# Two scheduling edits in a sparse masked attention kernel: projection units at an even step across the turns of the batch pairs, and the first query block of batches 0 and 1 computed in the last pair's slots

## The chip, the cores and the metric

The kernel runs on one NeuronCore of a Trainium2 chip, in one launch. The metric is device microseconds of one execution, the median of several runs. All data is float32, except for a bfloat16 mask bias of one block.

## The reference, cut to what matters

The input `x` is 8 batches of 2048 rows by 256 columns, `adj` a 2048 x 2048 sparse matrix whose first rows and columns are by far the fullest. Layer 0 is a graph convolution with two linear maps and two batch norms, a residual and a layer norm. Layer 1, which the change concerns, is attention masked by `adj`:

```python
qkv = h @ W                                  # 256 -> 3 x 256
q, k, v = ...                                # 4 heads of 64
mask = where(adj == 0, -inf, 0.0)
scores = einsum('bhid,bhjd->bhij', q, k) / sqrt(64) + mask
out = softmax(scores) @ v
# layer 1
x = _layernorm(x + out, axis=-1)
```

## The kernel before

Layer 0 ends at 957 us of the profiled execution with its output `y_d` in DRAM, not yet normalized. Everything below is `attention()`.

**Batches go in four pairs** (0 and 1, 2 and 3, and so on). A pair needs two kinds of work.

The first is **projection**, in 8 *units* of 512 rows, `(b, c)`: two batches of four chunks. A unit loads `y` and `x` (`load`, two SP DMAs of 512 KB each), applies the second batch norm (`bn`, ACT), turns `y` on the PE (`turn_y`), adds it to `x` and takes layer norm statistics (`norm`, DVE), makes scale and shift (`root` on POOL, `shift` on DVE), applies them (`apply`, ACT), turns the result (`turn` on PE, `turned` on ACT), and multiplies by the weights in four tiles of 128 rows (`keys_values`, `queries`). ACT copies the products out of PSUM (`took_keys_values`, `took_rows`). `store` (SP) writes 1032 KB of keys and values to `kv_d[p]` and 512 KB of queries to `q_d[p]`, one DRAM tensor of each for each pair.

Within a unit lies the pair's **first-block** work. The first 128 query rows of a batch are attended densely, as their rows of `adj` are the fullest. `first_queries` makes those queries transposed in `q0`, whose other halves POOL sets to zero by `memset`. Then for each of the unit's tiles: `turn_keys`, `turned_keys`, `scores0` (a mask bias and two products, PE), `exps0` (ACT), `weigh` (products with the values, added up in the one PSUM tile `po0` over the 16 tiles of a batch). At the end of a batch come `finish` (DVE), `residual` (POOL) and `out_stats` (DVE) for block 0.

The second is the **group loop**, for the query blocks `t` of 1 to 15. There are 132 groups in a pair, 528 in all. For each, POOL gathers 128 rows of keys and values of both batches (`gather`, `kg`, 528 KB) and, in 40 of 132 groups, 128 rows of queries (`qg`). DVE multiplies and reduces (`score`: `pr`, then `s`), ACT takes exponentials (`exps`, `pw`), `weigh_values` multiplies the values by them (`wv`; on ACT in two of five groups, in the last pair in three of five; else on DVE), and PE adds up (`add_up`, into `po`). After the last group of a block come `finish`, `residual` and `out_stats`, and after every fourth block `out_root`, `out_shift` and `emit`, which writes 512 KB of output.

The order on all five engines is the program's order, engine by engine; nothing is rearranged. Group `n` has a *slot* in which `score(n + 5)`, `exps(n + 4)`, `weigh_values(n + 3)`, `add_up(n)` and `gather(n + 10)` are issued, and behind them what is planned for the slot: the dictionary `slots` for projection of the next pair, `later` for the ends of blocks.

- Pair 0 is projected ahead of the loop, with `projection(0, 9)`: units follow at a step of 9 slots, which there are only an order, as no groups lie between.
- In pair p's 132 slots, pair p + 1 is projected with `projection(p + 1, 14)`: unit k begins at slot 14k, so that its last product is in slot 118 and its last `store` in slot 120. The first gather of pair p + 1 is in slot 122 and reads what the stores wrote.
- The last pair's slots hold no projection.

`kg` has 10 buffers, `wv` 5, `pr` 2, `x1` (the residual rows, kept from `load` to `emit`) 15, `ps_m` (PSUM for all of projection) 4, `ps_o` (for `po`) 3.

Of the kernel before, what the change touches and what calls it, by code (L numbers as in the profile page):

```python
# [8 lines left out]
F32 = mybir.dt.float32  # L9
# [4 lines left out]
AF = mybir.ActivationFunctionType  # L14
# [24 lines left out]
def tile_gcn_then_masked_attention(  # L39
# [15 lines left out]
    nc = tc.nc  # L55
    ENG = mybir.EngineType
    PSUM = bass.MemoryType.PSUM
    P = 128
    B, N, D = x.shape
    H = w1t.shape[1]  # L60
    O = w2t.shape[1]
    HD = D // NHEADS
# [790 lines left out]
    def rows(b, k, src, n=CH):  # L853
        return src[b, k * n : (k + 1) * n, :].rearrange("(t p) d -> p t d", p=P)
# [39 lines left out]
    def attention():  # L894

        with ExitStack() as st:
# [7 lines left out]
            x1, yt, x1t, ln, lo, kvr, qr, kt, q0, s0, p0, po0, zs, pms = ({} for _ in range(14))  # L904
# [58 lines left out]

            def first_queries(b):

                pm = pms["q0", b] = ps_m.tile([P, HP, P], F32, name="pm")
                for hp in range(HP):
                    for d in range(ND):
                        nc.tensor.matmul(
                            pm[:, hp, :], wq[:, d, hp * P : (hp + 1) * P], x1t[b, 0][:, d, :P],  # L970
                            start=(d == 0), stop=(d == ND - 1),
                        )
                q0[b] = ip.tile([P, HP, 2, P], F32, name="q0")
                for r in range(2):
                    nc.gpsimd.memset(q0[b][(1 - r) * HD : (2 - r) * HD, :, r, :], 0.0)

            def took_queries(b):
                pm = pms.pop(("q0", b))
                for r in range(2):
                    rs = slice(r * HD, (r + 1) * HD)  # L980
                    nc.scalar.activation(q0[b][rs, :, r, :], pm[rs], AF.Copy, scale=HD**-0.5)
# [97 lines left out]
            def residual(b, t):  # L1079
                c, i = divmod(t, TPC)  # L1080
                xt = x1[b, c]
                nc.gpsimd.tensor_add(xt[:, i, :], zs.pop((b, t)), xt[:, i, :])  # L1082

            def out_stats(b, t):
                c, i = divmod(t, TPC)
                if not i:
                    lo[b, c] = LayerNorm(ip, x1[b, c], "lo", 8)
                lo[b, c].stats([i])

            def out_root(b, c):  # L1090
                lo[b, c].root(range(TPC))

            def out_shift(b, c):
                lo[b, c].shift(range(TPC))

            def emit(b, c, half):
                lo[b, c].apply(range(IT * half, IT * (half + 1)))
                if half:
                    del lo[b, c]
                    nc.sync.dma_start(rows(b, c, out), x1.pop((b, c)))  # L1100

            def projection(p, step):

                slots = {}

                def at(s, f, *args):
                    slots.setdefault(s, []).append((f, args))

                units = [(b, c) for b in range(p * G2, (p + 1) * G2) for c in range(NCH)]
                for k, (b, c) in enumerate(units):  # L1110
                    s = k * step
                    at(max(0, s - step), load, b, c)
# [9 lines left out]
                    if not c:  # L1122
                        at(s + 9, first_queries, b)
                        at(s + 10, took_queries, b)
                    for i in range(TPC):
                        u = s + 9 + (step * i) // TPC
                        at(u, keys_values, b, c, i)
                        at(u + 1, took_keys_values, b, c, i)
                        at(u + 1, queries, b, c, i)
                        at(u + 2, took_rows, b, c, i)  # L1130
                        at(u + 2, turn_keys, b, c, i)
                        at(u + 3, turned_keys, b, c, i)
                        at(u + 4, scores0, b, c, i)
                        at(u + 5, exps0, b, c, i)
                        at(u + 7, weigh, b, c, i)
                    at(u + 3, store, b, c)
                    if c == NCH - 1:
                        at(u + 8, lambda b=b: finish(b, 0, po0.pop(b)))
                        at(u + 9, residual, b, 0)
                        at(u + 11, out_stats, b, 0)  # L1140
                return slots

            slots = projection(0, 9)
            for s in range(max(slots) + 1):
                for f, args in slots.get(s, ()):
                    f(*args)
# [32 lines left out]
            def score(n):  # L1179
# [3 lines left out]
                pr = ep.tile([P, G2, D], F32, name="pr")  # L1183
# [55 lines left out]
            def at(n, f, *args):  # L1239
                later.setdefault(n, []).append((f, args))  # L1240

            NALL_G = NP * NG
            for n in range(LEAD):
                gather(n)
# [6 lines left out]
            slots = {}  # L1251
            for n in range(NALL_G):
                p, g = divmod(n, NG)
                t, r, _, _ = tiles[g]
                if not g:
                    slots = projection(p + 1, 14) if p + 1 < NP else {}
# [11 lines left out]
                for f, args in slots.pop(g, ()):  # L1268
                    f(*args)
                for f, args in later.pop(n, ()):  # L1270
                    f(*args)
# [12 lines left out]
                assert g < NG - 1 or not slots  # L1284
            add_up(NALL_G - 1, 1)
            for n in sorted(later):
                for f, args in later[n]:
                    f(*args)
# [371 lines left out]
```

## Time and profile before

| | |
|---|---|
| Median of 3 runs | 2410.26 us (2410.09 to 2415.58) |
| The profiled execution's own time | 2455.75 us |
| Its span, from first to last instruction | 2453.9 us |
| Mean granted TensorE clock | 0.92 |
| Layer 1 begins (first `load`) | 957.8 us |
| First reduce of a score (`s`, L1186) of pair 0, 1, 2, 3 | 1152.2, 1482.8, 1819.1, 2151.0 us |
| Last reduce of a score | 2428.6 us |
| First gather (`kg`, L1168) of pair 0, 1, 2, 3 | 1144.9, 1474.8, 1811.2, 2143.5 us |

The table's lower half gives the stages: 194.4 us from the first load to the first score, then 330.6, 336.3, 331.9 and 277.6 us for the four pairs, then 25.3 us to the end. The profile is of one execution that is itself 45 us longer than the median; all sums over stages are in its time. Busy shares over the whole span mix layer 0, projection alone, loop with projection and loop without, so stages are read one by one.

### The profile page before, as it was taken

What the parts mean: (1) busy time and instruction counts of PE and PEld (TensorE: products, weight loads), DVE (VectorE), ACT (ScalarE), POOL (GpSimd) and SP (SyncE); (2) the same over time, 40 slices, a digit from 0 to 9 for tenths busy, and PEclk for the clock granted to TensorE, in tenths of its full rate; (3) what the DMA queues carried; (4) which work ended last, traced back from release to release, by engine and by line L of the source; (5) the groups of instructions that cost most, each with busy time, mean ns of one, the idle gap of its engine ahead of it and who ended that gap; (6) DMA issues with size and microseconds to landing.
All of it is one profiled execution on the core that took longest, in us unless ns stands there. A gap on an engine that the chain in (4) does not pass through costs nothing.

```text
span 2453.9 us, 28310 instructions
## 1 busy us (share of the span) xinstructions
PE 2089.6 (85%) x7860; PEld 1329.2 (54%) x7860; DVE 1911.3 (78%) x3650; ACT 1267.7 (52%) x3817; POOL 1480.1 (60%) x1497
## 2 busy tenths in 40 slices
PE   5898989888889997997899996999978999956654
PEld 1443434344434443775677774677756777744443
DVE  6977988778896665112888988888988889889996
ACT  6221111111105553554667776677757777767775
POOL 3405767576226774002767777667777668688784
PEclk7898999899899998998999998999989999978777
DMA  7868799697546743335879989899998899889995
GB/s 304 307 228 337 265 321 351 234 332 279 193 161 272 265 158 133 130 112 196 311 286 352 350 305 322 314 341 325 339 332 324 301 355 358 306 298 314 341 321 171
DMA packets 236152, 689.99 MB, mean 281 GB/s; under 512 B 25680, under 2 KB 91728, under 8 KB 213456
## 3 DMA queue, kind: packets, MB, share of 16 engines
q0 software_dynamic: 109248, 442.68, 50.5%
q1 hardware_dynamic: 124432, 228.62, 25.5%
q10 hardware_dynamic: 2304, 16.78, 1.7%
q8 instruction: 65, 1.06, 0.2%
q14 instruction: 103, 0.84, 0.1%
HBM read 557.19 MB, written 130.81 MB: 280 GB/s over the span
## 4 chain that ended last, share of the span: by engine, by line
PE 44%; DVE 14%; issue 7%; POOL 7%; ACT 5%; DMA 2%; another core or an unknown queue 1%; DVEq 0%; ACTq 0%; POOLq 0%; SPq 0%
PE pm L986 11%; PE po L1226 9%; PE pa L737 7%; DVE pr L1184 4%; PE pm L1035 3%; PE po L1054 3%; POOL kg L1168 3%; PE pa L645 3%; PE ph L498 2%; DVE s L1186 2%; ACT wv L1210 2%; DVE wv L1215 2%; ACT x L887 1%; DMA qg<-q_d,idxq 1%; POOL qg L1174 1%
## 5 line engine op out<-in xcount | busy, mean ns | idle before, releaser
L1168 POOL DMA_INDIRECT kg<-kv_d,idx x528 | 568.3, 1076 | 183.9 <-issue 107.7
L1226 PE MATMUL po<-wv,ident 128*128 128x260 f32 x1472 | 439.5, 416 | 173.5 <-DVE z L1075 87.5
L1210 ACT ACTIVATE wv<-kg,pw 128x65 f32<-128x65 f32 x1896 | 478.5, 338 | 8.8 <-remote 3.3
L1226 PEld LDWEIGHTS po<-wv,ident 128*128 128x128 f32 x1472 | 288.5, 207 | 264.1 <-issue 135.9
L1186 DVE TENSOR_REDUCE s<-pr 128x8 f32<-128x512 f32 x528 | 362.2, 686 | 34.6 <-ACT pw L1195 0.2
L986 PE MATMUL pm<-wq,x1t 128*128 128x512 f32 (+1 forms) x1024 | 377.8, 493 | 0.0
L645 PE MATMUL pa<-e,wt 128*128 128x512 f32 x536 | 264.8, 644 | 20.6 <-DVE e L353 13.0
L1184 DVE TENSOR_TENSOR pr<-qb,kg 128x512 f32<-128x512 f32 x368 | 257.3, 699 | 10.2 <-DMA kg<-kv_d,idx 9.6
L1195 ACT ACTIVATE pw<-s,padb 128x8 f32<-128x8 f32 x528 | 157.0, 300 | 201.4 <-DVE s L1186 163.3
L1215 DVE TENSOR_TENSOR wv<-kg,pw 128x520 f32<-128x520 f32 x291 | 214.0, 735 | 49.0 <-PE po L1226 20.2
L986 PEld LDWEIGHTS pm<-wq,x1t 128*128 128x128 f32 x1024 | 188.8, 192 | 82.3 <-issue 67.7
L1226 PE MATMUL po<-wv,oh 128*128 128x260 f32 x640 | 209.3, 427 | 10.3 <-DVE wv L1215 6.1
L1174 POOL DMA_INDIRECT qg<-q_d,idxq x160 | 161.0, 1006 | 48.8 <-issue 47.6
L645 PEld LDWEIGHTS pa<-e,wt 128*128 128x128 f32 x536 | 108.0, 208 | 151.4 <-issue 123.2
L1082 POOL TENSOR_TENSOR x<-z,x 128x256 f32<-128x256 f32 x128 | 122.8, 961 | 98.5 <-DVE z L1075 85.7
L563 POOL DMA_INDIRECT e<-xs_d,idx x116 | 125.2, 1079 | 81.5 <-PE pa L645 35.3
L309 POOL DMA_INDIRECT av<-in_adj_dram,fidx x116 | 134.6, 1161 | 47.8 <-issue 28.7
L1226 PEld LDWEIGHTS po<-wv,oh 128*128 128x128 f32 x640 | 133.4, 216 | 43.7 <-issue 12.4
L374 ACT COPY e<-ph 128x512 f32<-128x512 f32 x32 | 18.6, 582 | 249.1 <-PE ph L369 188.4
L931 DVE TENSOR_TENSOR x<-pm,x 128x512 f32<-128x512 f32 x64 | 43.9, 686 | 127.7 <-PE pm L925 116.3
L1054 PEld LDWEIGHTS po<-kvr,p 128*128 128x128 f32 x1024 | 137.0, 196 | 10.5 <-issue 3.8
L1035 PE MATMUL pm<-q,kt 128*128 128x256 f32 x512 | 133.7, 384 | 1.9 <-ACT kt L1023 1.9
(202 smaller groups left out, 3757.9 us busy)
## 6 DMA issues: line engine op xcount, KB each, us to landing
kv_d<-kvr SPq DMA_DIRECT2D x32, 1032.0 KB
e<-h_d SPq DMA_DIRECT2D x28, 1024.0 KB
e<-in_adj_dram SPq DMA_DIRECT2D x16, 1024.0 KB
xt<-in_x_dram SPq DMA_DIRECT2D x16, 1024.0 KB
xs_d<-xt ACTq DMA_DIRECT2D x16, 1024.0 KB
y_d<-y SPq DMA_DIRECT2D x32, 512.0 KB
yt<-y_d SPq DMA_DIRECT2D x32, 512.0 KB
x<-in_x_dram SPq DMA_DIRECT2D x32, 512.0 KB
```

Of the source, the lines that this page charges most:

```text
L645: nc.tensor.matmul(pa[c], w, xg[n].t[:, c * CH : (c + 1) * CH], start=(k == 0), stop=(k == count - 1),)
L737: nc.tensor.matmul(py, w[:, f, :], t[:, f, :], start=(f == 0), stop=(f == 1))
L986: nc.tensor.matmul(pm, x1t[b, c][:, d, i * P : (i + 1) * P], rhs(d), start=(d == 0), stop=(d == ND - 1),)
L1035: nc.tensor.matmul(pm[:, hp].rearrange("p r q -> p (r q)"), k[:, hp, :], q0[b][:, hp].rearrange("p r q -> p (r q)"), start=False, stop=Tru ...
L1054: nc.tensor.matmul(po0[b][:, h, :], p[:, h, :], heads(kvr[b, c][:, i, D:])[:, h, :], start=(j == 0 and h == 0), stop=(j == NT - 1), skip_g ...
L1168: nc.gpsimd.indirect_dma_start(out=kg[n].rearrange("p b e -> p (b e)"), out_offset=None, in_=kv_d[p][:], in_offset=bass.IndirectOffsetOnAx ...
L1174: nc.gpsimd.indirect_dma_start(out=qg[n].rearrange("p b e -> p (b e)"), out_offset=None, in_=q_d[p][:], in_offset=bass.IndirectOffsetOnAxi ...
L1184: nc.vector.tensor_mul(pr, q, kg[n][:, :, :D])
L1186: nc.vector.tensor_reduce(s.rearrange("p b h -> p (b h)"), pr.rearrange("p b (h e) -> p (b h) e", e=HD), AX.X, ALU.add,)
L1210: nc.scalar.activation(wv[n][:, b, hs], k[:, b, D:][:, hs], AF.Copy, scale=w[:, b, h : h + 1],)
L1215: nc.vector.tensor_mul(wv[n].rearrange("p b (h e) -> p b h e", e=VW), k[:, :, D:].rearrange("p b (h e) -> p b h e", e=VW), w[:, :, :, None ...
L1226: nc.tensor.matmul(po[p, t, b].rearrange("p h e -> p (h e)"), oh[n] if e >= 0 else ident, wv[n][:, b, :], start=(r == 0), stop=(r == ELL[t ...
```

## The change

1. `projection` takes a list of starting slots and plans into the one dictionary `later`, which now also has slots below 0 (in order, ahead of the loop). Pair 0's units start at slots -80, -74, ... -38, a step of 6. The units of pair p (1 to 3) start at `(p - 1) * 132 + int(88 - 16.5 * (7 - k))`: -27, -11, 5, 22, 38, 55, 71 and 88 within the pair's stretch, so 16 or 17 slots apart, and without a pause from one pair to the next. The last store is in slot 112 where it was in slot 120. `load` comes 8 slots ahead of a unit instead of one step.
2. The first 10 gathers are issued in slot -19, behind the last store of pair 0 (slot -22) and among the first unit of pair 1, whose `first_queries`, with the `memset` of `q0`, is in slot -18.
3. Pair 0 is projected without first-block work. `left_over` does that work later, from slot 382 (14 slots before the last pair's first) in steps of 15 slots: each unit's keys and values are read back from `kv_d[0]` (`read_keys_values`, 1032 KB), the 128 query rows of each batch from `q_d[0]` (`read_queries`, 128 KB) and turned on the PE (`turn_queries`), then `first_block` as before. It is done by slot 516.
4. Because the output rows of block 0 of batches 0 and 1 are then late, POOL copies their residual rows aside (`keep_rows`, into `rest`), `emit` leaves them out, and `emit_rest` writes them.
5. `pr` goes from 2 buffers to 1.

Its core (the parts that only pass names along are left out):

```diff
+            def keep_rows(b):
+                rest[b] = ip.tile([P, 1, D], F32, name=f"rest{b}", bufs=1)
+                nc.gpsimd.tensor_copy(rest[b][:, 0, :], x1[b, 0][:, 0, :])
+
+            def read_keys_values(b, c):
+                kvr[b, c] = ip.tile([P, TPC, KW], F32, name="kvr")
+                g = b % G2
+                nc.sync.dma_start(
+                    kvr[b, c],
+                    kv_d[b // G2][c * CH : (c + 1) * CH, g * KW : (g + 1) * KW].rearrange(
+                        "(t p) e -> p t e", p=P
+                    ),
+                )
+
+            def read_queries(b):
+                g = b % G2
+                zs[b, "q"] = ip.tile([P, D], F32, name="z", bufs=4)
+                nc.sync.dma_start(zs[b, "q"], q_d[b // G2][:P, g * D : (g + 1) * D])
+
+            def turn_queries(b):
+                pm = pms["q0", b] = ps_m.tile([P, HP, P], F32, name="pm")
+                rows_q = zs.pop((b, "q"))
+                for hp in range(HP):
+                    nc.tensor.transpose(pm[:, hp, :], rows_q[:, hp * P : (hp + 1) * P], ident)
+                open_queries(b)
...
+            def first_block(at, u, b, c, i):
+
+                at(u, turn_keys, b, c, i)
+                at(u + 1, turned_keys, b, c, i)
+                at(u + 2, scores0, b, c, i)
+                at(u + 3, exps0, b, c, i)
+                at(u + 5, weigh, b, c, i)
+                if c == NCH - 1 and i == TPC - 1:
+                    at(u + 6, lambda: finish(b, 0, po0.pop(b)))
+                    at(u + 7, residual, b, 0)
+                    at(u + 9, out_stats, b, 0)
+
+            def left_over(at, s0, step):
+
+                for k, (b, c) in enumerate((b, c) for b in range(G2) for c in range(NCH)):
+                    s = s0 + k * step + 6
+                    at(s - 6, read_keys_values, b, c)
+                    if not c:
+                        at(s - 6, read_queries, b)
+                        at(s - 2, turn_queries, b)
+                        at(s - 1, took_queries, b, 1.0)
+                    for i in range(TPC):
+                        first_block(at, s + (step * i) // TPC, b, c, i)
...
-            def projection(p, step):
+            def projection(at, p, starts, step, ahead):
...
-                for k, (b, c) in enumerate(units):
-                    s = k * step
-                    at(max(0, s - step), load, b, c)
+                for s, (b, c) in zip(starts, units):
+                    at(s - ahead, load, b, c)
...
-                    if not c:
+                    if p and not c:
                         at(s + 9, first_queries, b)
...
-                        at(u + 2, turn_keys, b, c, i)
-                        at(u + 3, turned_keys, b, c, i)
-                        at(u + 4, scores0, b, c, i)
-                        at(u + 5, exps0, b, c, i)
-                        at(u + 7, weigh, b, c, i)
+                        if p:
+                            first_block(at, u + 2, b, c, i)
...
-                pr = ep.tile([P, G2, D], F32, name="pr")
+                pr = ep.tile([P, G2, D], F32, name="pr", bufs=1)
...
+            NUNITS = G2 * NCH
+            FIRST, STEP0, LAST = -80, 6, 88
+            steady = NG / NUNITS
+            projection(at, 0, [FIRST + STEP0 * k for k in range(NUNITS)], STEP0, STEP0)
+            for p in range(1, NP):
+                starts = [
+                    (p - 1) * NG + int(LAST - steady * (NUNITS - 1 - k)) for k in range(NUNITS)
+                ]
+                projection(at, p, starts, int(steady), 8)
+            left_over(at, (NP - 1) * NG - 14, 15)
+            GATHER = FIRST + STEP0 * NUNITS + 13
...
+            for n in range(min(later), 0):
+                side_tasks(n)
+                if n == GATHER:
+                    for m in range(LEAD):
+                        gather(m)
```

## The prediction, on record before the change was run

> **What bounds the kernel now.** I read the layer 1 stages one by one, first by a table of stretches: the first pair's projection alone, then the four pairs between the first score of each and the next (columns: length, then busy time of PE, PE weight loads, DVE, ACT and POOL, granted clock, DMA share, GB/s).
>
> ```profile
> 1000.00:1050.00 50.00, 50.00 (x262) 37.19 (x261) 10.46 (x33) 26.78 (x65) 4.86 (x20) 1.00 0.33 110
> 1050.00:1100.00 50.00, 50.00 (x269) 37.92 (x268) 8.71 (x26) 30.39 (x73) 3.53 (x13) 1.00 0.37 126
> ...
> 1700.00:1750.00 50.00, 49.60 (x242) 38.48 (x241) 47.35 (x98) 41.53 (x142) 39.81 (x49) 1.00 1.02 387
> ```
> ```profile
> 1152.00:1483.00 331.00, 297.60 (x1388) 227.70 (x1389) 288.07 (x589) 233.26 (x800) 232.43 (x264) 0.95 0.90 326
> 1483.00:1819.00 336.00, 300.99 (x1409) 232.08 (x1409) 293.81 (x607) 238.83 (x816) 238.50 (x273) 0.95 0.91 328
> 1819.00:2151.00 332.00, 296.95 (x1409) 228.06 (x1408) 293.39 (x608) 237.79 (x816) 241.07 (x272) 0.97 0.91 326
> 2151.00:2429.00 278.00, 168.27 (x528) 123.78 (x526) 252.41 (x485) 198.61 (x783) 219.13 (x215) 0.75 0.91 312
> ```
>
> Projection alone is PE and nothing else: 50 of 50 us, DVE and DMA mostly idle. In the first three pairs, PE, DVE and DMA are all near 90%; in the last, DVE and DMA still are, while PE has over 100 us to spare. The chain that ended last, in order of time, shows the unit's beat (time, length, work):
>
> ```profile
> 985.55 2.58 PE pm L986 x8
> ...
> 1006.29 2.58 PE pm L986 x8
> ...
> 1027.03 2.58 PE pm L986 x8
> ```
>
> A unit takes 20.74 us. Later in the chain the same work returns at 1373.56 and 1443.44, four half units or 28 slots apart: 69.9 us, 2.50 us a slot. Last, the timelines of POOL and DVE where the loop begins (start, length):
>
> ```profile
> 1144.89 1.09 POOL L1168 DMA_INDIRECT kg<-kv_d,idx  x1 [0.16 <-issue]
> ...
> 1162.00 0.94 POOL L1168 DMA_INDIRECT kg<-kv_d,idx  x1 [0.30 <-issue]
> ```
> ```profile
> 1151.51 0.69 DVE L1184 TENSOR_TENSOR pr<-qb,kg 128x512 f32<-128x512 f32 x1 [6.11 <-DMA kg<-kv_d,idx]
> ```
>
> PE's projection ends near 1140; the stores land, the first ten `kg` with four `qg` take POOL 18 us, and DVE starts 12 us after PE's end.
>
> **What the skill says.** The Trainium skill, "Perfetto Trace Analysis", section Optimization Strategy: where regimes with different most-contended engines follow one another, interleaving them may help. That is the table above. The section Identifying the Most-Contended Engine says that matmul busy time misleads, since matmuls are pipelined; here the groups of the first projection sum to 208 us of matmul in a stretch of 178, so I price PE by start to start. "VectorE: DVE Perf Modes", The DRAIN you can't avoid: a wait between two DVE operations is free. The trace differs: a reduce and the multiply behind it, without a wait, are 0.60 us apart, a multiply and the reduce that waits for it 0.72. "DMA: Bandwidth & Descriptors", Issuing engines are not separate DMA queues: all share the 16 engines, so SP's re-reads compete with POOL's gathers.
>
> **Prices on PE**, start to start at full clock, from the trace's starts: 512 columns 0.43 us, 256 columns 0.216, mask bias 0.216, transposes 0.109, 65 columns 0.105. Projection proper of a unit: 16 x 0.43 + 16 x 0.216 + 16 x 0.109 = 12.1 us. First-block work: 8 x 0.109 + 4 x 0.216 + 16 x 0.216 + 32 x 0.105 = 8.55, and 0.9 for `first_queries` of a batch. Together 20.9 on average, against a beat of 20.74. A group's four `add_up` records: 4 x 0.219 = 0.88.
>
> **Step 1, the start.** Taken from the PE-bound stretch: 8 x 8.55 + 2 x 0.9 = 70.2 us. Put into it, from pair 1: the whole unit of slot -27 (20.9) and of the unit at -11 the turns and the first tile (1.7 + 2.6). Net -45 us. Short units have less filler (ACT needs 9.5 of every 12.1 us): I add 5 (0 to 12). Alone this puts PE's end at 1100, and as the first gathers now overlap with pair 1's unit, the first score at about 1103.
>
> A new wait stands against that. Slot -19 puts the gathers ahead of slot -18's `memset` of `q0` on POOL, and `scores0` in slot -14 needs it. Pair 0's last product comes at 985.5 + 8 x 12.1 - 9 (done by then) + 5 = 1078. From the last store's issue (1138.55) to the first gather (1144.89) it was 6.3 us, so the gathers start near 1087 and hold POOL for 18 us, to 1105. PE gets to `scores0` near 1087 and stands until 1106. Behind it in PE's order are `turn_y` of the next unit and so its `norm`, which DVE must do ahead of the first score. The first score comes at about 1116. Bounds: 1103 if nothing is waited for, 1127 if stores land late and the short units cost 12. I take 1116: **gain 36** (25 to 49).
>
> **Step 2, the first three pairs.** Spread evenly, PE needs 20.8 / 16.5 + 0.88 = 2.14 us a slot; at 14 slots it was 20.8 / 14 + 0.88 = 2.36 and took 2.50. So PE at the same efficiency would run at 2.26. DVE was busy for 875 us in 396 groups and keeps that, but for 1.4 units of 3.3 us that move ahead; at the 94.5% of its fullest window it needs 870 / 0.945 = 921, or 2.33 a group. DMA: 0.91 x 2.52 = 2.29. So DVE comes next, close above the others, and three in-order queues so near each other lose more than one: I take 2.39, so 946 us for the present 999: **gain 53** (30 to 75). The pause at each pair's end (132nd gather at 1466.1, next at 1474.8, where 2.4 us is usual) goes with it, as the last store is in slot 112 and the gather that needs it in 122.
>
> **Step 3, the last pair.** Added: PE 8 x 8.55 + 1, or 69 us, into more than 100 of slack. ACT: eight times 4 x (0.37 + 0.59) = 31 us, beside 199 of 278. DVE: two `finish` and `out_stats`, 2.4 us, which the start no longer has. SP: 8 re-reads of 1032 KB and 2 of 128, at 387 GB/s for a share of 1.02 some 22 us of DMA time; the share is 0.91 of 278, so it fits if the gathers leave no holes, and I charge 8 (0 to 22). POOL: four `memset` of 0.3 us. The two 0.7 us copies and the output writes of the rows kept apart are too small to show. The wait at this pair's start saves 5. **Loss 3** (gain 5 to loss 17). The work ends in slot 516 of 528, so the 25 us behind the last score stay.
>
> **Step 4, one `pr`.** A multiply may have to wait for the reduce before it, at 0.72 to 0.78 instead of 0.60. Only 71 of 528 multiplies follow the reduce directly; elsewhere another operation lies between. 71 x 0.18 = 13 at most, nothing if no wait is set. I take **5**. Step 2's cover, DVE, is full, so this is paid.
>
> **Sum:** 36 + 53 - 3 - 5 = 81 us, on a span of 2453.9. The profiled execution (2455.75) is 1.9% longer than the median of the runs shown (2410.26), so 81 becomes 79: **2331 us**. The parts' bounds do not all fall on one side: 2298 to 2366.
>
> **Rivals.**
> - *The loop does not speed up*, since PE was not what held it: DVE and DMA are as full as PE in the table. Then only steps 1 to 4 without 53 remain, and with 8 more for fuller DMA in the last pair: 36 - 3 - 5 - 8 = 20, 2390. Against it: 2.10 us a group in the last pair at the same DMA share.
> - *Everything fits*: no wait at the start (49), DVE at 94.5% throughout (78), nothing lost in the last pair: 127 less, 2285. For it: 1700 to 1750, where DVE, PE and DMA are all full at once.
> - *Slower: gather packets lengthen.* The place is the 16 DMA engines in the loop. From the queue part of the page, 50.5% of 16 x 2453.9 us over 109,248 packets is 181 ns a packet; one ns on the loop's 528 x 128 `kg` packets is 4.2 us. The loop needs 0.91 x 1276 + 22 = 1183 us of engine time. To end 7 us behind today, with 36 gained at the start, it would have to last 1276 + 36 + 7 = 1319, which takes 136 us more, or 32 ns a packet: from 213 ns on. For it: the last pair moves only 312 GB/s at 0.91. Against: 387 GB/s at 1.02 where most was asked.
> - *No change*: start and loop both at the poor end and re-reads in the way; the sum of bounds just reaches it.
>
> **How the numbers follow.** The forecast 0.66, the loop unchanged 0.13, everything fits 0.12, slower 0.06, no change 0.03. Under 0.3%, some 7 us, a measurement of this kernel can't tell from none. Faster: 0.66 + 0.13 + 0.12 = 0.91; within 0.3% 0.03; slower 0.06. The range, 2292 to 2374, holds the forecast whole and a part of the two neighbours.
>
> **What would show it.** Right: first score near 1116, with PE idle some 20 us after 1087 and released by POOL's `memset`; the same beat of about 39 us a unit through three pairs; 132nd and 133rd gather no further apart than others; pair lengths near 315; the last pair near 280, clock near 1.0 there, DMA share near 1. Wrong: pairs still at 330, with DVE waiting for `kg`; PE waiting for `x` of `apply`; SP late with `qb`; or the last pair over 300.

## The result and the profile after

| | before | after |
|---|---|---|
| Median of 5 runs, same chip | 2411.19 us (2410.09 to 2415.58) | 2390.99 us (2381.67 to 2396.34) |
| Ratio, 95% interval | | 0.9903 (0.9873 to 0.9932) |
| Profiled execution, span | 2455.75, 2453.9 us | 2381.67, 2379.7 us |

The change makes the kernel 20 us faster. 79 had been forecast, and the result lies outside the range (2292 to 2374), next to the rival in which the loop does not speed up (2390).

The two profiles cannot be subtracted from each other. By their times they come from different chips: on the three chips of the runs below the unchanged kernel took 2410, 2450 and 2460 us. Below, ratios are to the kernel before on the same chip, and stages are compared on the two chips where it took 2450 (e5 to e8, e13 to e16) and 2460 us (e1 to e4, e9 to e12); e17 and e18 are from the one with 2410. The labels e1 to e18 name the runs.

The same table of stretches as before, first the start, then the four pairs (columns: length, busy time of PE, PE weight loads, DVE, ACT and POOL, granted clock, DMA share, GB/s):

```profile
945.00:1099.00 154.00, 123.99 (x482) 80.15 (x483) 38.77 (x123) 78.96 (x187) 30.60 (x82) 0.89 0.59 206
1099.00:1429.00 330.00, 295.28 (x1387) 226.08 (x1385) 288.58 (x590) 231.48 (x800) 223.91 (x255) 0.96 0.88 318
1429.00:1760.00 331.00, 300.77 (x1411) 232.32 (x1412) 292.81 (x609) 238.00 (x817) 236.75 (x273) 0.96 0.90 332
1760.00:2075.00 315.00, 281.36 (x1319) 216.99 (x1317) 287.88 (x585) 228.66 (x793) 235.23 (x262) 0.96 0.93 344
2075.00:2356.00 281.00, 212.94 (x1003) 170.58 (x1003) 254.81 (x493) 222.55 (x848) 223.94 (x221) 0.92 0.93 333
```

The start is 154 us where it was 194. The first two pairs still take 330 us, on a faster chip, the third 315, and in the first two PE and DVE are as busy as before. So the start gave what was forecast and the loop nearly nothing. In the start, the chain in order of time shows pair 0's short units:

```profile
965.89 9.46 PE pm L1015 x28
...
977.96 9.46 PE pm L1015 x28
...
990.03 9.46 PE pm L1015 x28
```

That is 12.07 us a unit, against the 12.1 worked out. Then the timelines of POOL and of PE (start, length, idle time before it) show the forecast wait:

```profile
1065.29 1.09 POOL L1228 DMA_INDIRECT kg<-kv_d,idx  x1 [2.26 <-DMA kv_d<-kvr]
...
1081.67 0.94 POOL L1228 DMA_INDIRECT kg<-kv_d,idx  x1 [0.30 <-issue]
1082.65 0.67 POOL L967 MEMSET q<- 64x256 f32 x2
```
```profile
1083.37 2.07 PE L1064 MATMUL pm<-q,kt 128*128 128x256 f32 x4 [12.27 <-POOL kvr L1026]
```

The `memset` of `q0` stands behind the fourteen gathers, and `scores0` waits for it (the line names the `memset` right behind it, L1026, but PE starts 0.05 us after the one of `q0` has ended). In the loop a wait appears that DVE did not have in the profile before. DVE's waits from the first score to the last (total, times, longest):

```profile
DVE pr L1244 <- DMA qb<-q_d: 42.4, 12, 9.4
DVE lo_nm L881 <- POOL lo_rs L141: 15.1, 11, 2.6
DVE wv L1275 <- PE po L1286: 7.5, 4, 2.3
```

`qb` holds the query rows of a block, 256 KB, which SP fetches in `load_q` when the block's first gather is issued. The DMA issues (KB each, median us from issue to landing):

```profile
yt<-y_d SPq DMA_DIRECT2D x32, 512.0 KB, 11.5
x<-in_x_dram SPq DMA_DIRECT2D x32, 512.0 KB, 15.8
...
qb<-q_d SPq DMA_DIRECT2D x60, 256.0 KB, 14.0
```

Of the 53 `qb` whose landing the trace tells, the 15 issued in the loop within 6 us behind a unit's two stores and another unit's two loads (1032 + 512 + 512 + 512 KB on SP) landed 16 to 23 us later, 20.7 in the median. The first two, behind the same burst but with the gathers only just beginning, took 6.3 and 5.7. The 24 with no `store`, `load` or re-read in those 6 us took 4 to 21, 11.5 in the median, so the burst is not all that delays a `qb`. At a step of 16 or 17 slots and a load 8 slots ahead, `load` of the unit after next falls directly behind `store`: slot s + 25 behind s + 24.

### The profile page after: what moved, and what is told of

Its sections match the earlier page's. It is cut to its first block, busy times and chain, and to the rows that moved or that the text cites. A ratio compares the mean times of both kernels' runs of the same rounds, so it can differ in the third digit from the quotient of the medians.

```text
span 2379.7 us, 28412 instructions
## 1 busy us (share of the span) xinstructions
PE 2057.4 (86%) x7848; PEld 1310.8 (55%) x7848; DVE 1910.7 (80%) x3652; ACT 1262.0 (53%) x3817; POOL 1475.2 (62%) x1503
## 3 DMA queue, kind: packets, MB, share of 16 engines
q0 software_dynamic: 109248, 442.68, 50.9%
## 4 chain that ended last, share of the span: by engine, by line
PE 28%; DVE 21%; DMA 12%; issue 7%; ACT 6%; POOL 5%; DVEq 0%; SPq 0%; ACTq 0%; POOLq 0%
PE pa L737 8%; DMA qb<-q_d 7%; DVE pr L1244 6%; PE pm L1015 6%; PE po L1286 4%; DVE wv L1275 3%; DVE s L1246 3%; ACT wv L1270 3%; PE pa L645 3%; PE ph L498 2%; DMA qg<-q_d,idxq 2%; POOL kg L1228 2%; PE pm L1064 1%; DVE ln_st L871 1%; DVE x L931 1%
## 5 line engine op out<-in xcount | busy, mean ns | idle before, releaser
L1286 PE MATMUL po<-wv,ident 128*128 128x260 f32 x1472 | 427.8, 401 | 101.0 <-DVE z L1104 97.1
L1015 PE MATMUL pm<-wq,x1t 128*128 128x512 f32 (+1 forms) x1024 | 370.7, 493 | 0.4 <-ACT x1t L960 0.4
L1286 PEld LDWEIGHTS po<-wv,ident 128*128 128x128 f32 x1472 | 273.4, 198 | 173.4 <-issue 121.9
L645 PE MATMUL pa<-e,wt 128*128 128x512 f32 x536 | 255.8, 625 | 24.4 <-DVE e L353 17.1
L1015 PEld LDWEIGHTS pm<-wq,x1t 128*128 128x128 f32 x1024 | 195.7, 193 | 96.5 <-issue 74.6
L1275 DVE TENSOR_TENSOR wv<-kg,pw 128x520 f32<-128x520 f32 x291 | 211.1, 725 | 11.5 <-PE po L1286 7.5
L1286 PE MATMUL po<-wv,oh 128*128 128x260 f32 x640 | 204.6, 409 | 12.1 <-DVE oh L1261 7.5
L1234 POOL DMA_INDIRECT qg<-q_d,idxq x160 | 166.0, 1038 | 48.8 <-issue 46.0
L1064 PE MATMUL pm<-q,kt 128*128 128x256 f32 x512 | 142.2, 402 | 43.5 <-ACT kt L1052 31.0
L1286 PEld LDWEIGHTS po<-wv,oh 128*128 128x128 f32 x640 | 122.2, 203 | 40.7 <-issue 12.4
L1064 PEld LDWEIGHTS pm<-q,kt 128*128 128x128 f32 x512 | 99.2, 199 | 80.8 <-ACT kt L1052 43.6
L1111 POOL TENSOR_TENSOR x<-z,x 128x256 f32<-128x256 f32 x126 | 113.7, 904 | 43.0 <-DVE z L1104 35.4
## 6 DMA issues: line engine op xcount, KB each, us to landing
yt<-y_d SPq DMA_DIRECT2D x32, 512.0 KB, 11.5
```

Source lines behind the costliest of these rows:

```text
L645: nc.tensor.matmul(pa[c], w, xg[n].t[:, c * CH : (c + 1) * CH], start=(k == 0), stop=(k == count - 1),)
L1015: nc.tensor.matmul(pm, x1t[b, c][:, d, i * P : (i + 1) * P], rhs(d), start=(d == 0), stop=(d == ND - 1),)
L1064: nc.tensor.matmul(pm[:, hp].rearrange("p r q -> p (r q)"), k[:, hp, :], q0[b][:, hp].rearrange("p r q -> p (r q)"), start=False, stop=Tru ...
L1234: nc.gpsimd.indirect_dma_start(out=qg[n].rearrange("p b e -> p (b e)"), out_offset=None, in_=q_d[p][:], in_offset=bass.IndirectOffsetOnAxi ...
L1275: nc.vector.tensor_mul(wv[n].rearrange("p b (h e) -> p b h e", e=VW), k[:, :, D:].rearrange("p b (h e) -> p b h e", e=VW), w[:, :, :, None ...
L1286: nc.tensor.matmul(po[p, t, b].rearrange("p h e -> p (h e)"), oh[n] if e >= 0 else ident, wv[n][:, b, :], start=(r == 0), stop=(r == ELL[t ...
```

## The experiments

Two theories stood first. **A:** the query rows come late, since SP now issues 2.6 MB ahead of them, and this takes back the loop's gain. **B:** the loop is full, and a wait that is removed comes back elsewhere.

### Late query rows

The kernel before again, for its stages on that chip (e1):

> The kernel before, unchanged, for a second profile with landing times and at its usual speed (the first profile was 45 us over the median). Theory A (in the changed kernel the query rows qb come late, because SP issues a store of 1.5 MB and a load of 1 MB directly ahead of them): here loads and stores of projection are 6 to 8 slots apart, so qb lands within some 8 us in the median and DVE waits for it under 8 us in all. Theory B (the DMA engines are simply full and qb is only the first to show it): qb lands as late as in the changed kernel, 14 us in the median. For both: span near 2410, and the stages that are shorter than in the first profile show where its 45 us were.

Measured: 2459.5 us; start 194.2, pairs 329.3, 338.6, 334.0 and 279.4. Not 2410: the other eleven runs of this kernel on that chip took 2448 to 2468, so the 45 us of the first profile are a chip's, not one execution's. DVE waits for `qb` 0.6 us in all, as theory A had it. When `qb` landed, the traces of e1 to e4 do not tell, so DVE's waits decide.

`load_q` four groups earlier, all else as in the changed kernel (e2):

```diff
-                if not r:
-                    load_q(p, t)
...
+            def queries_ahead(n):
+                p, g = divmod(n, NG)
+                if not tiles[g][1]:
+                    load_q(p, tiles[g][0])
...
+                if n + LEAD + 4 < NALL_G:
+                    queries_ahead(n + LEAD + 4)
```

> The changed kernel with qb loaded 4 groups (some 9 us) earlier. Theory A: DVE's wait for qb falls from 42 us to under 8, and the time falls by 30 to 42 us, to some 2355. Theory B: the wait moves to kg or elsewhere, and the time falls by less than 10.

Loads 16 slots ahead of a unit instead of 8, which parts them from the stores (e3):

```diff
-                projection(at, p, starts, int(steady), 8)
+                projection(at, p, starts, int(steady), 16)
```

> The changed kernel with a unit's loads issued 16 slots ahead instead of 8, so that they lie 7 slots in front of a store instead of directly behind one. Theory A: qb lands in 8 to 12 us instead of 14 to 20 behind a store, DVE's wait for it falls from 42 to under 15, and the time falls by 20 to 35 us. Theory B: landing and time as they were, within 10.

Both (e4):

> The changed kernel with both: qb 4 groups earlier and loads 16 slots ahead. Theory A: no more than 5 us better than the better of the two alone, since both remove the same wait. Theory B: as the changed kernel, within 10; or, if fuller buffers help in general, the gains of the two add up.

Measured, ratios to before: 0.9809 (0.9784 to 0.9834), 0.9835 (0.9811 to 0.986) and 0.9812 (0.9788 to 0.9837). The changed kernel itself was run again (e5) beside a further version (e6), with `qb` early as in e2, in which also the zeros of `q0` of pair 1's first batch are written ahead of the first gathers:

```diff
                 if n == GATHER:
+                    open_queries(G2)
                     for m in range(LEAD):
```

> The changed kernel as it is, on the same chip as the runs beside it; ratios to the kernel before are what is compared. Theory A (the late query rows cost the loop its gain): 0.990 as in the result, with VectorE waiting 40 us or so for qb, and the version with query rows fetched 4 groups earlier 0.8 to 1% below it. Theory B (the engines' coupling is the limit, the query rows only one of its forms): 0.984 to 0.990, within 0.3% of the version with earlier query rows, since the wait comes back at wv. In both, pairs 0 and 1 take 330 us or more.

> The changed kernel with the query rows fetched 4 groups earlier, and the zeros of q0 of the first batch of pair 1 written before the first ten gathers instead of behind them. If the wait of TensorE for the memset (12.3 us in the profile after) delays the first score, the start shrinks from about 154 us by 6 to 12 us and the ratio to before is 0.976 to 0.979. If the first score waits for the gathers anyway, TensorE's idle time moves to another place, the start stays at 154 us and the ratio at 0.981.

| stage, us | before (e1) | after (e5) | qb and memset earlier (e6) |
|---|---|---|---|
| first load to first score | 194.2 | 153.6 | 149.6 |
| pairs 0, 1, 2 | 329.3, 338.6, 334.0 | 340.0, 351.9, 324.1 | 329.2, 330.7, 317.9 |
| last pair | 279.4 | 289.2 | 290.3 |
| ratio | | 0.9926 (0.9905 to 0.9946) | 0.979 (0.9766 to 0.9813) |

The changed kernel lost 14 us in its first three pairs (1016.0 against 1001.9), and the version with early `qb` and `memset` took 38 off them (977.8). These are single profiles, e1 from another chip than e5 and e6; by the medians, less what start and last pair gave, the loss is some 15 and the later gain some 35. That late `qb` is the cause is shown twice: by fetching it earlier (e2, DVE no longer waits for it), and by parting loads and stores (e3), which leaves `load_q` alone. DVE's wait for `qb` in e1, e5 and e3:

```profile
DVE pr L1184 <- DMA qb<-q_d: 0.6, 2, 0.3
...
DVE pr L1244 <- DMA qb<-q_d: 46.9, 8, 8.9
...
DVE pr L1244 <- DMA qb<-q_d: 5.7, 3, 3.5
```

Against the ratio of e5, e2 is worth 29 us and e3 22, and both at once (e4) no more. But theory B holds too. With `qb` early, DVE's largest waits in the loop (e2) are

```profile
DVE wv L1278 <- remote: 36.7, 11, 6.1
DVE lo_nm L881 <- POOL lo_rs L141: 14.9, 12, 2.6
DVE x L931 <- PE pm L925: 14.5, 7, 4.2
```

and in e6 pairs 0 and 1 stand at 329 and 331, where the kernel before took 329 and 339. `wv` waits for buffers that PE frees ("remote" stands for a releaser that the trace does not name).

The `memset` was worth 4 us of start, not the 6 to 12 expected. POOL and PE in e6 say why:

```profile
1069.94 0.66 POOL L967 MEMSET q<- 64x256 f32 x2
...
1088.51 0.94 POOL L1227 DMA_INDIRECT kg<-kv_d,idx  x1 [0.30 <-issue]
1089.45 0.22 POOL L1027 MEMSET kvr<- 128x4 f32 x4
```
```profile
1089.62 1.97 PE L1084 MATMUL po<-kvr,p 128*128 128x65 f32 x8 [7.32 <-POOL kvr L1027]
```

The next `memset` in POOL's order, the ones in `kvr`, is behind the gathers too, and PE waits for that one 7.3 us.

### The two parts of the change, each alone

Even projection alone (e9): pair 0 keeps its first blocks in the start, at a step of 9 slots, and the gathers come behind them.

```diff
-                    if p and not c:
+                    if not c:
                         at(s + 9, first_queries, b)
...
-                        if p:
-                            first_block(at, u + 2, b, c, i)
+                        first_block(at, u + 2, b, c, i)
...
-            left_over(at, (NP - 1) * NG - 14, 15)
-            GATHER = FIRST + STEP0 * NUNITS + 13
+            GATHER = -14
```

> One part of the change alone: the projections of pairs 1 to 3 evenly over the slots (16.5 slots a unit, beginning 27 slots before the pair before starts), pr with one buffer; the first blocks of batches 0 and 1 stay in the start, as in the kernel before, and the first ten gathers stay behind them. Theory A (the even beat is worth little because VectorE's own work, 289 to 294 us a pair with 0.905 of the time in use at best, is the next limit, and the late query rows take back what is left): pairs 0 and 1 within 1.5% of before, or longer, pair 2 shorter by 8 to 16, the last pair as before (279), the start longer or equal (194 to 210, as work of pair 1 has moved in front): ratio 0.997 to 1.012. Theory B (the even beat is where the result's 20 us come from): ratio 0.990.

First blocks in the last pair alone (e10): the other pairs' projections at 14 slots, from slot 0.

```diff
-                starts = [
-                    (p - 1) * NG + int(LAST - steady * (NUNITS - 1 - k)) for k in range(NUNITS)
-                ]
-                projection(at, p, starts, int(steady), 8)
+                starts = [(p - 1) * NG + 14 * k for k in range(NUNITS)]
+                projection(at, p, starts, 14, 14)
```

> The other part alone: first-block attention of batches 0 and 1 in the last pair, short start, first gathers right behind the stores; the projections of pairs 1 to 3 keep 14 slots a unit from slot 0 of the pair before, as in the kernel before; pr with one buffer. Theory A: the start is shorter by 55 to 70 us than 194 (no unit of pair 1 moved in front of it), pairs 0 to 2 as before within 1% plus 2 to 3 us each for the one pr buffer, the last pair 10 to 14 us longer than 279: ratio 0.979 to 0.987, as good as the whole change or better. Theory B: the two parts share the gain, and this one alone gives 0.990 or more.

| stage, us | before (e1) | even alone (e9) | first blocks alone (e10) | both, qb early (e2) |
|---|---|---|---|---|
| first load to first score | 194.2 | 214.3 | 127.6 | 154.3 |
| pairs 0, 1, 2 | 329.3, 338.6, 334.0 | 340.3, 351.0, 328.9 | 329.9, 342.0, 340.9 | 335.3, 335.4, 322.4 |
| last pair | 279.4 | 274.9 | 295.2 | 294.4 |
| ratio | | 1.010 (1.007 to 1.013) | 0.9832 (0.9799 to 0.9865) | 0.9809 (0.9784 to 0.9834) |

In both runs theory A of its expectation had the ratio right; of its stages the start (e9) and the last pair (e10) came out a few us longer than stated, and pair 2 gained 5 where 8 to 16 were expected (e9). The even projection alone makes the kernel *slower* by 1%, late query rows included (DVE waits 31 us for `qb` in e9, 4 in e10). The first blocks alone make it faster by 1.7%, which is more than the whole change gives. Even with its query rows mended, the even beat adds nothing that can be told from zero: 0.9809 against 0.9832, and with the `memset` early too 0.979 (e6), all with intervals that overlap. It shortens the third pair by some 18 us (322.4 against 340.9), as units have left its slots for those of the pair before, and pays with 20 to 27 us of start, where pair 1's first units now stand.

### What holds the loop

If coupling held it (DVE never more than a slot ahead of PE), more `wv` buffers should free it. The version e6 with seven instead of five, and 14 `x1` buffers to make room (e7):

> As the run with query rows and memset earlier, with seven wv buffers instead of five (and 14 x1 buffers instead of 15 to make room). If the loop is held by coupling, VectorE being unable to run more than one slot ahead of TensorE because the wv buffers come free one group late, then VectorE's wait at wv (18 to 23 us per pair) goes and pairs 0 and 1 drop from 335 to 315 us or so, the total by 30 to 50 us. If TensorE or VectorE is the limit by its own work, the wait is only named differently: pairs 0 and 1 stay within 4 us of the version with five buffers.

Measured 0.9765 (0.9747 to 0.9783); pairs 329.0, 331.7, 316.7 and 285.0. DVE's waits for PE moved from `wv` to `x` and `inv_all`, and pairs 0 to 2 stayed: coupling through `wv` is not their limit. The last pair took 5 us less.

Then each resource was cut by itself, on e6, in kernels that leave out a part of the sums or of the data. TensorE by its products, where the loop over the width runs over half of it (e8):

```diff
-                for d in range(ND):
+                for d in range(ND // 2):
...
-                        start=(d == 0), stop=(d == ND - 1),
+                        start=(d == 0), stop=(d == ND // 2 - 1),
```

> As the run with query rows and memset earlier, but the projections for keys, values and queries sum over half of the model's width: one 128x512 and one 128x256 matmul less for each of the four tiles of a unit, 0.645 us a tile, 2.58 us a unit, 20.6 us of TensorE's time in a pair of eight units; all other instructions stay. If TensorE's work is the limit of pairs 0 and 1, both drop by 18 to 21 us and the second by 16. If VectorE is the limit, they stay within 4 us. If the two hold each other up, about half: 8 to 13 us. The start, which TensorE alone sets, drops by some 20 us in all cases.

The 20.6 us there are half of the truth. A product has four matmuls in the trace, two of which go, so the cut is 41 us a pair. The start became 21 us shorter, as stated, but by luck: 41 had been taken from it too. VectorE by its sums (e11), the base again (e13), and the DMA engines by the gathers (e15, in which the keys and values of each batch lie in a DRAM tensor of their own):

```diff
-                    pr.rearrange("p b (h e) -> p (b h) e", e=HD), AX.X, ALU.add,
+                    pr.rearrange("p b (h e) -> p (b h) e", e=HD)[:, :, : HD // 2], AX.X, ALU.add,
```

> The changed kernel with query rows and memset earlier, but VectorE's reduce adds up 32 of the 64 products of a head: about 0.27 us less in each of 528 reduces, some 36 us of VectorE's work in a pair; everything else stays. If VectorE is the limit of the loop: pairs 0 and 1 drop from 330 by 25 to 36 us, the last from 290 likewise. If TensorE is the limit (it has 277 to 282 us of work in pairs 0 and 1): pairs 0 and 1 drop by less than 6, the last, where TensorE has 183, by 20 or more. If both are close to their limits and hold each other up: 8 to 20 in pairs 0 and 1.

> The version with query rows and memset earlier once more, as the base for the three runs beside it on the same chip. Pairs 329 to 336, 330 to 336, 317 to 322, 290 to 294; ratio to before 0.979.

```diff
-                kg[n] = ep.tile([P, G2, KW], F32, name="kg", bufs=LEAD)
+                kg[n] = ep.tile([P, 1, KW], F32, name="kg", bufs=LEAD)
```

> As the base, but each gather fetches one batch's keys and values (2,064 bytes a row for 4,128) and both batches of the pair use them: 35 MB less in a pair of 105; instructions of the engines stay in number and size. Theory D (the DMA engines are the third holder of the loop, beside TensorE and VectorE): pairs 0 and 1 drop by 8 to 20, the last by 10 to 20. Rival (TensorE and VectorE alone hold each other up): pairs 0 to 2 stay within 4 us, though the last may drop.

and then in company (e16, e17, e18):

> As the base, with both cuts at once: projections over half the width (TensorE 41 us less a pair) and sums over 32 of 64 products (VectorE 26 to 30 us less). Alone they took 14, 6, 7 and 13, 10, 10 us off pairs 0 to 2. If the two engines alone hold each other up, both cuts together take more than the sum: pairs 0 and 1 at 285 to 298. If a third resource holds the loop right behind them, they take no more than the larger of the two alone and a few us: 305 to 316.

> The version with query rows and memset earlier, with two cuts at once: each gather fetches one batch's keys and values for both batches of the pair (35 MB less a pair), and the reduce adds 32 of 64 products (VectorE 26 to 30 us less a pair). Alone they took 4 and 1 to 3 us off the last pair and 6 to 8 and 10 to 13 off pairs 0 and 1. If the DMA engines and VectorE stand right behind each other in the last pair, both cuts take 20 us or more off it (from 290 to 270 or less), and pairs 0 and 1, where TensorE stays, drop to 302 to 312. If TensorE's and ScalarE's alternation in the last pair's first blocks sets it, it stays at 282 to 290.

> As the one with two cuts, and the projections over half the width as well (TensorE 41 us less in pairs 0 and 1). If three resources of nearly equal load hold the loop, only all three cuts free it: pairs 0 and 1 at 265 to 290, where two cuts (products and sums) left 311 to 313. If something else stands behind them (ScalarE, the order of the queues), pairs 0 and 1 stay at 295 to 310. The last pair, where the products play no part, is as with two cuts.

| cut | pairs 0, 1, 2 | last pair | ratio |
|---|---|---|---|
| none (e13) | 329.0, 332.3, 316.9 | 291.8 | 0.9768 (0.9723 to 0.9813) |
| PE, 41 us a pair (e8) | 315.0, 324.7, 311.4 | 291.3 | 0.9608 (0.9584 to 0.9631) |
| DVE, 25 to 30 us (e11) | 315.9, 320.8, 307.6 | 288.8 | 0.9589 (0.9557 to 0.9621) |
| DMA, 35 of 105 MB (e15) | 322.8, 324.5, 313.4 | 288.2 | 0.9713 (0.9686 to 0.9741) |
| PE and DVE (e16) | 313.1, 311.2, 298.8 | 284.5 | 0.9426 (0.9393 to 0.9459) |
| DMA and DVE (e17) | 301.0, 300.9, 291.8 | 280.2 | 0.9536 (0.952 to 0.9552) |
| all three (e18) | 290.0, 295.8, 289.6 | 280.5 | 0.9368 (0.9351 to 0.9386) |

The last two rows are from a faster chip (before 2410), where the base was not run; the profile after, in which the changed kernel has pairs of 330, 330, 316 and 281, is of a chip like it. No single cut returns more than a half of itself in pairs 0 to 2, and PE's cut about a third or less. The DMA cut lies between theory D (8 to 20 us in pairs 0 and 1) and its rival (under 4): 6 and 8 us, where a run that leaves these pairs alone (e14, below) gave 4 and 4, and its ratio overlaps the base's. It shows better in company: 0.9426 becomes 0.9368 with it, and 0.9589 becomes 0.9536, some 13 us each time.

By the ratios the cuts add up. Alone they take 0.016, 0.018 and 0.0055 off the base's 0.9768. PE and DVE together take 0.034, DMA and DVE 0.023, all three 0.040: the sums, within the intervals. e16's pairs 0 and 1 lie where a third resource was expected to stand, but over its three pairs it takes 55 us off the base, for 27 and 34 alone: neither more than the sum nor just the larger. No one queue hides the others in pairs 0 to 2; each cut returns its part of itself, whatever else is cut. (e17 and e18, in us of another chip, decide nothing by their pairs: 290 and 296 in e18 stand at the border of its two expectations.) And no cut, nor all three, brings the last pair below 280. One more run had asked the DMA engines there, with six of eight re-reads left out (e14):

```diff
+                if c:
+                    kvr[b, c] = kvr[b, 0]
+                    return
                 kvr[b, c] = ip.tile([P, TPC, KW], F32, name="kvr")
```

> As the base, but in the last pair the first blocks of batches 0 and 1 read their first 512 rows of keys and values from memory once and use them four times: six of eight re-reads left out, 6.2 MB, some 18 us of DMA time at the 348 GB/s that a full share gives there; TensorE, ScalarE and VectorE do all that they did. Theory D (the DMA engines set the last pair, which is why 36 us less of VectorE's work took only 1.5 us from it): the last pair drops from 290 by 8 to 18. Rival E (TensorE's and ScalarE's first-block work in the slots sets it): within 3 us of the base. Pairs 0 to 2 stay.

It gave 292.5 against 291.8: theory D falls for the last pair. Pairs 0 to 2, which it leaves alone, came out at 325.4, 328.8 and 318.4, so a difference of 4 us between two single profiles says nothing. What is left in the last pair is shown by the groups of POOL with three cuts, from 1951 to 2232 us (busy time, mean ns of one, idle time before them and what ended it):

```profile
L1227 POOL DMA_INDIRECT kg<-kv_d,idx x128 | 141.9, 1109 | 33.5 <-issue 19.7 <-ACT pw L1259 3.7 <-ACT wv L1274 2.3
L1233 POOL DMA_INDIRECT qg<-q_d,idxq x39 | 41.8, 1072 | 11.9 <-issue 11.3 <-DMA qg<-q_d,idxq 0.6
L1112 POOL TENSOR_TENSOR x<-z,x 128x256 f32<-128x256 f32 x30 | 29.3, 978 | 0.5
```

and by POOL's waits in the same stretch:

```profile
POOL kg L1227 <- issue: 19.7, 81, 0.3
POOL qg L1233 <- issue: 11.3, 37, 0.3
POOL kg L1227 <- ACT pw L1259: 3.7, 13, 0.3
```

No wait is longer than 0.3 us, whatever it is put down to. Each gather takes 1.1 us of busy time in the mean and 0.3 us ahead of it that counts as idle. Busy time is 227 us and the short gaps 47; POOL's last instruction begins 6.6 us before the last score, which makes 280. **POOL never stops**: the issue of gathers is the floor. And it was so before the change; POOL's waits in the last pair of the kernel before:

```profile
POOL kg L1168 <- issue: 26.0, 97, 0.8
POOL qg L1174 <- issue: 11.3, 37, 0.3
POOL kg L1168 <- ACT pw L1195: 4.0, 13, 0.3
POOL x L1082 <- DVE z L1075: 1.6, 2, 1.2
```

There gaps, as far as each goes beyond 0.35 us, sum to 2.5 us of 278. In pairs 1 and 2 of e18 they sum to 2.9 of 295.8 and 2.2 of 289.6, so with all three cuts POOL has become the floor of these pairs too; in pair 0 it still waits 11.6 of 290.0. That POOL holds the last pair follows from its unbroken queue and from the other cuts' failure; a run with less work on POOL was not made.

The floor is not POOL's alone. In the timeline of the kernel before, a gather that begins while DVE multiplies (into `pr` or `wv`) takes longer than one that begins during a reduce:

```profile
2199.36 0.69 DVE L1184 TENSOR_TENSOR pr<-qb,kg 128x512 f32<-128x512 f32 x1
2199.73 1.13 POOL L1168 DMA_INDIRECT kg<-kv_d,idx  x1 [0.30 <-issue]
...
2200.95 0.69 DVE L1215 TENSOR_TENSOR wv<-kg,pw 128x520 f32<-128x520 f32 x1
2201.17 1.29 POOL L1168 DMA_INDIRECT kg<-kv_d,idx  x1 [0.30 <-issue]
...
2203.67 0.69 DVE L1186 TENSOR_REDUCE s<-pr 128x8 f32<-128x512 f32 x1
2204.01 0.94 POOL L1168 DMA_INDIRECT kg<-kv_d,idx  x1 [0.30 <-issue]
```

In the whole loop of the profile after, all 164 `kg` gathers of over 1.1 us began within such a multiply; the 248 that began outside one took 1.09 us at most. So it is in e6, e13 and e18 too. In the last pair the 72 begun within a multiply took 18 us more than at 0.94 us each (21 in e18), which is the part of the floor that goes with DVE's multiplies. No run was made that takes these multiplies away.

### The best version

In e12, room from `x1` (14 buffers) spent on six `wv` and again two `pr`; in the last pair's first blocks one slot more ahead of `scores0` and of `weigh`; with e6's two edits.

```diff
-                at(u + 2, scores0, b, c, i)
-                at(u + 3, exps0, b, c, i)
+                at(u + 2 + lag, scores0, b, c, i)
+                at(u + 3 + lag, exps0, b, c, i)
+                u += 2 * lag
                 at(u + 5, weigh, b, c, i)
...
-                pr = ep.tile([P, G2, D], F32, name="pr", bufs=1)
+                pr = ep.tile([P, G2, D], F32, name="pr")
```

> Query rows and memset earlier, 14 x1 buffers, and with the room so found six wv buffers and two pr buffers again; in the last pair's first blocks one slot more between the key turn and the scores and one more between the exponentials and the weighing. If one pr buffer costs 0.117 us at each of 67 multiplies that directly follow a reduce, that is 8 us back over the loop, if VectorE is the limit there; if TensorE's waits for ScalarE (31 us at the scores, 16 us at the weighing, in the last pair) are what lengthens the last pair to 290, that pair falls to 278 to 284. Ratio 0.968 to 0.974. If both are hidden behind other waits: 0.977 to 0.979, as without them.

Measured 0.9719 (0.969 to 0.9748): it beats both kernels, the changed one by 2% (0.9926 in e5). The ratio is as expected; which of the edits of e12 gave how much was not run apart. In the trace most of 66 multiplies directly behind a reduce are back at 0.603 us from start to start, where they took 0.720. In the last pair PE's lost time at `scores0` fell from 32 us (e6) to 14 and at `weigh` from 17 to 6 (start to start, above the prices), and yet the pair took 287.4, not 278 to 284: the second half of the expectation failed, since PE was not what held that pair.

## Why the prediction was right or wrong

- **Step 1, the start, held.** Gain 41 (194.2 to 153.6) for 36 forecast. The unit's price was exact (12.07 us for 12.1). The POOL wait was there, 12.3 us long for some 20; the gathers began 119 us after the first load where 129 was worked out, and the first score came 34 us behind them, not 29.
- **Step 2, the first three pairs, failed.** 53 us of gain was forecast; the changed kernel lost 14 there, and with `qb` and `memset` early gained 24 (e6; 9 to 19 in the single profiles e2 to e4), mostly the work that had moved out of the third pair. Two terms of the step were wrong.
  - *A queue was left out.* The step priced PE, DVE and DMA share and never asked what SP has in front of `load_q` once loads and stores fall together. "SP late with `qb`" stood among the signs of failure, without a price. It cost 38 us in single profiles (e5 against e6), some 22 to 35 by the medians.
  - *The ceiling was taken from the best 50 us.* "94.5% of its fullest window" (47.35 of 50 is 94.7) gave DVE 2.33 us a group, and 2.39 with 0.06 for queues so near each other. With `qb` mended the loop ran at 977.8 / 396 = 2.47. PE, DVE and DMA were at 87 to 91% already over a whole pair, and the even beat did not make PE wait less: above its work at the prices of the prediction (277.8, 282.9 and 282.0 us in pairs 0 to 2) the kernel before spent 52, 56 and 52 us (e1), the one with `qb` mended 52, 48 and 53 (e6, with 277.4, 282.7 and 265.0 of work). That several in-order queues hold these pairs together is what the cuts show; by which order of waits each loses its part stays open.
- **The rate of the last pair was put down to DVE and DMA.** It was POOL's, hidden by the busy column (219 of 278), since the gap ahead of each gather is not busy. As evidence against the rival "the loop does not speed up", its 2.10 us a group was the least that POOL allows there; it does not show that DVE could keep it in the other pairs.
- **Step 3, the last pair,** was sized at 3 and cost 10 (279.4 to 289.2), within its bounds. The reason given, DMA time for the re-reads, is refuted by e14. POOL's gaps beyond 0.35 us sum to 14 us there (e13), against 3 (e1), and its busy time to 223 against 220: with the first blocks it waits for DVE and ACT now and then.
- **Step 4, one `pr`,** held in its price: 67 multiplies at 0.720 instead of 0.603 are 7.8 us of DVE's time, for 5 forecast and 13 as the bound. What of it reaches the kernel's time was not measured by itself.
- **Rivals.** "The loop does not speed up" was right in that PE was not the loop's only holder, and its 2390 near the result, in part by luck: it had 36 - 3 - 5 - 8 with the loop unchanged, and the stages of e1 and e5 give 41 - 14 - 10 and 1 at the end. "Gather packets lengthen" did not happen: 50.9% of 16 x 2379.7 us over 109,248 packets is 177 ns, for 181 before (179 in e5, on a chip of the slower kind).
- **Signs.** The pause at a pair's end went (8.74 us between the 132nd and 133rd gather, now 1.85). The beat is 41 us a unit in pairs 0 and 1, not 39; in the profile after, the clock in the last pair 0.92 and the DMA share 0.93, not near 1.

## What to carry to other kernels

In this kernel, spreading work evenly gained nothing: it can pay only where a queue stands idle at one time that is needed at another. Price the evened stage from each queue's whole-stage share, gaps ahead of its instructions included, not from the busiest window. When a step is moved, list for every issuing queue what now stands directly in front of a small transfer or a small `memset` that someone waits for.

## What was not expected of the hardware

- A gather holds POOL some 1.25 us where DVE is idle (the start) and 1.4 in the mean in the loop; 0.3 of it are not shown as busy. So 128 gathers and 39 of queries with the rest of POOL's work fill 274 us (e18).
- Every `kg` gather of the loop that took longer than 1.1 us (164 in the profile after, 207 in e18) began while DVE was multiplying into `pr` or `wv`.
- A 256 KB read behind 2.6 MB on the same issuing engine landed in 16 to 23 us while the gathers ran, and in 6.3 and 5.7 while they had hardly begun.
- The same kernel differs by 2% between chips (2410 to 2460 us), at granted clocks that hardly differ: 0.927 to 0.930 in the runs on the fast chip, 0.916 to 0.929 on the two others.
